# Borders between the stages of two bottleneck layers: statistics ahead and by rows, a first norm on two engines, a plain first tile, stores in parts

## The chip, the cores and the metric

The kernel runs on one core of a Trainium2 chip. Time is the device time of one execution in microseconds. The core has five engines with their own instruction streams: TensorE (PE, matmuls, with its weight loads shown as PEld), VectorE (DVE), ScalarE (ACT), GpSimd (POOL) and SyncE (SP). SP, ACT and POOL also issue DMAs. Matmuls write to eight banks of PSUM, everything else lies in SBUF or in DRAM.

## The reference

Two layers of the same form are applied to x, 64 images of 1024 channels and 14 x 14 pixels in float32. One layer is

```
out = relu(bn(conv(x,   w1, b1, 1, 0), g1, be1))    # 1x1, 1024 -> 256
out = relu(bn(conv(out, w2, b2, 1, 1), g2, be2))    # 3x3,  256 -> 256
out =      bn(conv(out, w3, b3, 1, 0), g3, be3)     # 1x1,  256 -> 1024
x   = relu(x + softplus(residual_scale)[0] * out)
```

where bn takes mean and variance over all images and pixels: gamma * (x - mean) * rsqrt(var + 1e-5) + beta. So each bn needs all of its convolution's output before its first element can be normalized.

## The kernel before

Channels lie on the 128 partitions: 1024 channels are 8 blocks (CS), 256 are 2 "slots" (MS). Pixels are cut into T = 32 tiles of two images (PX = 392 columns), and for conv2 into NG = 8 groups of eight images (1568 columns per slot). The 256 channels between the convolutions stay in SBUF for all images (`y_all`); x between the layers goes through DRAM (`mids`). A float32 matmul shows as two PE instructions in the profile.

The stages, with b the number of the layer:

1. *First stage* (b = 0): conv1, the first two tiles plainly (`plain_conv1`, L378), the others by a scheme of seven products for a 2 x 2 block multiplication (`Seven`, L170, `Conv1`, L236). `stream` (L213) orders the products p1..p7 of neighbouring tiles. DVE makes the sums t1, t2, t3 (L287 to L289) after p1 and t4 (L306) after p6; results go to `y_all` by ACT or by DVE (L279), with `bn_stats` (L282) per tile. x_0 comes in two halves.
2. *Border to conv2*: `aggregate` (L689) turns the 32 rows of statistics of each slot into mean and variance with one `bn_aggr` each, `affine` (L700 to L717) makes scale and shift: a square root on ACT, the rest small DVE operations. `norm` (L396) applies them on ACT with a relu, group by group.
3. *conv2*: in rows of images by a transform with six products (0 to 5), taken in the pairs (1,2), (3,4), (0,5) for each group. `combine` (L413 to L450) makes the inputs r of a pair and their column sums on DVE and loads transformed weights u (1280 KB) on SP's queue; `products` (L470 to L483) are the matmuls, first the one that reads `sums`; `finish` adds the results (L503, L534) and takes the `bn_stats` of the group by tiles of 392 columns when all four rows of outputs are written. `combine` of the next pair is called before `products` of this one.
4. *Border to gram*: `aggregate`, `affine`, `norm` as before; `crow`, a row of constants, is loaded by SP. For b = 0, w1 of the next layer is loaded by four issues on ACT (L109).
5. *gram* (L559): conv3's statistics are taken from Z'Z, so that conv3 need not run twice. In 49 steps of 256 columns Z is transposed on PE (L583), centred by DVE (L585), and multiplied (L571, L572). `conv3_stats` (L597) makes mean and variance of all 1024 outputs (`quad`, L632).
6. *Fused stage* (b = 0, `fused`, L649): conv3 of layer 0 by seven products (`Conv3`, L311, stream c, 28 products per tile) side by side with conv1 of layer 1 (stream a, 28 products per tile), one product of each in turn. c starts 28 + LAG = 42 products ahead. ACT copies product banks (L234), DVE adds them to x in place (L341), POOL adds others (L367), ACT applies relu and stores the tile on its own queue (L376).
7. For b = 1 conv2, gram, and then `residual` (L638) per tile: conv3 plainly, DVE (L645), ACT relu (L646), one store on POOL's queue. The first two conv3 blocks are `made` ahead of the statistics.

The order of matmuls on PE is the program's own (`keep_in_program_order`, L135). Some operations of DVE and ACT are held to it as well; the others are placed by a scheduler. Each engine works its instructions in that order; buffers come from pools, and PSUM banks carry names. In the fused stage the banks are ay (2), ap, ax for conv1 and cy (2), cp, cx for conv3. A product into a bank waits until what was in it has been read; p3 of a quad of conv3 goes into the bank cp that p5 filled, after DVE has read it (L341).

Of the kernel before, what the change touches and what calls it, by code (L numbers as in the profile page):

```python
# [21 lines left out]

# [49 lines left out]
def bottlenecks(ctx: ExitStack, tc: tile.TileContext, x, w1s, w2s, w3s, pars, out):  # L72
# [18 lines left out]
    def psum_pool(bufs=8):  # L91
        return tc.tile_pool(name="psum", bufs=bufs, space=bass.MemoryType.PSUM)
# [44 lines left out]
    def psum_tile(psum, n=PX, tag="ps", **kw):  # L137
        return psum.tile([P, 512], FP, tag=tag, name=tag, **kw)[:, :n]

# [30 lines left out]
    class Seven:  # L170
# [7 lines left out]
        def bank(self, tag, bufs=1):  # L178
            tag = self.prefix + tag
            return self.psum.tile([P, 512], FP, tag=tag, name=tag, bufs=bufs)[:, : self.n]  # L180

        def p1(self):
            self.y = self.bank("y", 2)
            yield from self.product(self.y, self.a[0][0], self.b[0][0], True)
            self.after1()
# [50 lines left out]
    class Conv1(Seven):  # L236
# [28 lines left out]
        def end(self):  # L265
            pass
# [17 lines left out]
        def after1(self):  # L284
            self.u1 = self.saved("au1")
            self.t1, self.t2, self.t3 = (self.sum(i) for i in range(1, 4))
            nc.vector.tensor_sub(self.t3, self.b[1][1], self.b[0][1])  # L287
            nc.vector.tensor_add(self.t2, self.t3, self.b[0][0])
            nc.vector.tensor_sub(self.t1, self.b[0][1], self.b[0][0])  # L289
# [88 lines left out]
    def plain_conv1(psum, t, xt, a, par, stats):  # L378

        banks = [psum_tile(psum) for o in range(MS)]  # L380
# [11 lines left out]
    def norm(g, aff):  # L392
        scale, shift = aff
        for s in range(MS):
            y = y_grp[:, s, g]
            nc.scalar.activation(y, y, AF.Relu, bias=shift[:, s : s + 1], scale=scale[:, s : s + 1])  # L396

    def conv2(psum, pool, b, par, aff, stats):
# [9 lines left out]
        def last(to, g, k, by):  # L408

            nc.scalar.activation(to[:, :, RT - 1, :], y_grp[:, :, g, 4 * (RT - 1) + k - 1, :], AF.Copy, scale=by)  # L410
# [4 lines left out]
        def combine(g, pair):  # L415

            full = RT - 1
            ra, rb = new("r"), new("r")
            if pair[0] == 1:
                t1, t2 = new("t"), new("t")  # L420
                last(t1, g, 2, -4.0)
                last(t2, g, 1, -4.0)
                for s in range(MS):
                    stt(t1[:, s, :full], rows(g, s, 2, 0, full), -4.0, rows(g, s, 4, 0, full))
                    stt(t2[:, s, :full], rows(g, s, 1, 0, full), -4.0, rows(g, s, 3, 0, full))
                nc.vector.tensor_add(ra, t1, t2)
                nc.vector.tensor_sub(rb, t1, t2)
            elif pair[0] == 3:
# [3 lines left out]
                both = slice(0, MS)  # L432
                nc.vector.tensor_sub(t3[:, :, :full], rows(g, both, 4, 0, full), rows(g, both, 2, 0, full))
                nc.vector.tensor_sub(t4[:, :, :full], rows(g, both, 3, 0, full), rows(g, both, 1, 0, full))
                stt(ra, t4, 2.0, t3)
                stt(rb, t4, -2.0, t3)
            else:
# [7 lines left out]
            made = []  # L445
            for i, r in zip(pair, (ra, rb)):
                lines = (full if i == NF - 1 else RT) * GI
                r = r.rearrange("p s r (i w) -> p s (r i) w", i=GI)[:, :, :lines]
                sums = pool.tile([P, MS, RT * GI, WH], FP, tag="sums", name="sums", bufs=BUFS["sums"])[:, :, :lines]
                nc.vector.tensor_add(sums, r[:, :, :, WH:], r[:, :, :, :WH])  # L450
                u = pool.tile([P, MS, MS, NK, P], FP, tag="u", name="u", bufs=BUFS["u"])
                nc.sync.dma_start(out=u, in_=us[b][i])
                made.append((i, lines, r, sums, u))
            return made

        def products(made):
            done = []
            for i, lines, r, sums, u in made:
# [3 lines left out]
                for o in range(MS):  # L462
                    def w(s, k):
                        return u[:, s, o, k]
# [80 lines left out]
        for k, (g, pair) in enumerate(pairs):  # L545
            if pair[0] == 1 and g + 1 < NG:
                norm(g + 1, aff)
# [318 lines left out]
```

## Time and profile before

| | us |
|---|---|
| median of 4 runs | 2213.17 (2212.88 to 2214.5) |
| the profiled execution, its time | 2214.5 |
| its span | 2212.7 |
| PE busy | 2128.6 (96%) |
| DVE busy | 1431.4 (65%) |
| ACT busy | 724.0 (33%) |
| POOL busy | 250.4 (11%) |
| mean granted TensorE clock | 0.982 |

A busy line gives an engine's time, its share of the span and its instructions. A wait line names the instruction that waited, and behind the arrow the one that released it, with total, times and longest. The chain of waits is the path of work followed back from the last instruction. A granted clock of 1.00 is full speed of TensorE. A single time such as 806.78 is counted from the start of the span.

### The profile page before, as it was taken

To read this page: it belongs to the slowest core of one execution; us is meant where nothing else is said; L and a number is where in the kernel's file an instruction comes from. 1 tells how busy PE (TensorE), PEld (TensorE's weight loads), DVE (VectorE), ACT (ScalarE), POOL (GpSimd) and SP (SyncE) were. 2 spreads that over 40 slices of the span, in tenths; PEclk is the share of its full clock that TensorE was granted. 3 is DMA by queue.
4 is the path that set the end of the run, shared out by engine and by line. 5 is a ranking of instruction groups with operands and counts; after the bars stand their busy time and mean duration, and the time that the engine had idled before them with its cause. 6 is when DMAs were issued, how large, how long until landed. Compare 5 with 4: busy or idle time off the path is not lost.

```text
span 2212.7 us, 27233 instructions
## 1 busy us (share of the span) xinstructions
PE 2128.6 (96%) x10648; PEld 1810.7 (82%) x10648; DVE 1431.4 (65%) x2591; ACT 724.0 (33%) x1391; POOL 250.4 (11%) x350
## 2 busy tenths in 40 slices
PE   8999979999998989999999999799999799999997
PEld 4555549999997879999999999699999797555554
DVE  5676557788775656676666666678878534444443
ACT  1111133111105045555555555611111221444443
POOL 0000000000001133333333333000000000000000
PEclk9999989999998989999999999899999899999999
DMA  7655425555534424444444442355555501787884
GB/s 283 251 201 202 174 96 181 187 199 184 187 137 158 153 94 170 175 175 165 165 167 175 175 175 117 148 190 191 190 187 194 195 16 55 295 292 295 306 318 185
DMA packets 44289, 409.44 MB, mean 185 GB/s; under 512 B 5504, under 2 KB 5760, under 8 KB 11392
## 3 DMA queue, kind: packets, MB, share of 16 engines
q1 hardware_dynamic: 29664, 287.06, 36.2%
q0 software_dynamic: 8448, 67.11, 7.4%
q10 hardware_dynamic: 6048, 53.52, 5.8%
q8 instruction: 84, 1.38, 0.3%
q14 instruction: 45, 0.37, 0.0%
HBM read 289.18 MB, written 118.49 MB: 184 GB/s over the span
## 4 chain that ended last, share of the span: by engine, by line
PE 73%; issue 20%; DVE 4%; DMA 2%; POOL 1%; ACT 1%; POOLq 0%; SPq 0%; ACTq 0%
PE ay L135 14%; PE cy L135 7%; PE ap L135 7%; PE ps L475 6%; PE ps L481 6%; PE ps L470 6%; PE ps L477 6%; PE ps L483 6%; PE cp L135 4%; PE ax L135 3%; PE cx L135 2%; PE bx L571 2%; PE ps L135 1%; DMA y<-in_w 1%; PE bp L572 1%
## 5 line engine op out<-in xcount | busy, mean ns | idle before, releaser
L135 PE MATMUL ps<-y,w 128*128 128x392 f32 x1024 | 339.2, 494 | 0.0
L135 PEld LDWEIGHTS ps<-y,w 128*128 128x128 f32 x1024 | 195.2, 191 | 142.8 <-issue 1.6
L645 DVE SCALAR_TENSOR_TENSOR x<-ps,scale,x 128x392 f32<-128x392 f32 x256 | 159.8, 625 | 174.2 <-PE ps L135 174.2
L234 ACT ACTIVATE cu<-cy,scale 128x196 f32<-128x196 f32 x384 | 158.4, 422 | 230.2 <-PE cy L135 227.7
L646 ACT ACTIVATE x<-x,shift 128x392 f32<-128x392 f32 x256 | 158.9, 622 | 177.5 <-DVE x L645 177.5
L135 PE MATMUL ay<-at,w1s 128*128 128x196 f32 (+1 forms) x752 | 209.7, 382 | 0.8 <-ACT au L234 0.6
L503 DVE TENSOR_TENSOR f<-ps,ms 128x448 f32<-128x448 f32 x192 | 113.3, 600 | 147.8 <-PE ps L483 80.2
L470 PE MATMUL ps<-sums,u 128*128 128x224 f32 (+1 forms) x768 | 172.1, 347 | 25.2 <-DVE sums L450 25.2
L475 PE MATMUL ps<-r,u 128*128 128x224 f32 (+1 forms) x768 | 173.6, 347 | 0.0
L481 PE MATMUL ps<-r,u 128*128 128x224 f32 (+1 forms) x768 | 172.8, 346 | 0.0
L494 ACT ACTIVATE ms<-ps 128x448 f32<-128x448 f32 (+1 forms) x80 | 41.9, 524 | 391.2 <-PE ps L470 391.2
L135 PEld LDWEIGHTS ay<-at,w1s 128*128 128x128 f32 x752 | 136.0, 190 | 36.3 <-ACT au L234 4.3
L470 PEld LDWEIGHTS ps<-sums,u 128*128 128x128 f32 x768 | 137.3, 190 | 26.2 <-ACT t L410 13.1
L234 ACT ACTIVATE x<-x,shift 128x392 f32<-128x392 f32 x256 | 145.5, 614 | 30.8 <-POOL x L367 28.9
L477 PE MATMUL ps<-r,u 128*128 128x192 f32 (+1 forms) x768 | 153.7, 321 | 0.0
L483 PE MATMUL ps<-r,u 128*128 128x192 f32 (+1 forms) x768 | 153.4, 321 | 0.0
L367 POOL TENSOR_TENSOR x<-x,cu 128x392 f32<-128x392 f32 x128 | 130.4, 1019 | 190.1 <-DVE x L341 187.8
L341 DVE SCALAR_TENSOR_TENSOR x<-cp,scale,x 128x196 f32<-128x196 f32 x256 | 106.8, 417 | 67.1 <-PE cp L135 67.1
L475 PEld LDWEIGHTS ps<-r,u 128*128 128x128 f32 x768 | 141.8, 190 | 1.3
L481 PEld LDWEIGHTS ps<-r,u 128*128 128x128 f32 x768 | 136.4, 188 | 1.4
L477 PEld LDWEIGHTS ps<-r,u 128*128 128x128 f32 x768 | 132.7, 189 | 1.2
L483 PEld LDWEIGHTS ps<-r,u 128*128 128x128 f32 x768 | 132.0, 188 | 1.1
(161 smaller groups left out, 3674.2 us busy)
## 6 DMA issues: line engine op xcount, KB each, us to landing
u<-u SPq DMA_DIRECT2D x96, 1280.0 KB, 5.5
x<-in_x SPq DMA_DIRECT2D x62, 1568.0 KB, 6.7
mid<-x ACTq DMA_DIRECT2D x32, 1568.0 KB, 5.1
x<-mid SPq DMA_DIRECT2D x32, 1568.0 KB, 8.3
out<-x POOLq DMA_DIRECT2D x32, 1568.0 KB, 8.4
u<-y POOLq DMA_DIRECT2D x24, 320.0 KB, 6.5
u<-spare POOLq DMA_DIRECT2D x24, 320.0 KB, 3.1
x<-in_x SPq DMA_DIRECT2D x4, 784.0 KB, 6.7
```

Of the source, the lines that this page charges most:

```text
L135: tc.keep_in_program_order(nc.tensor.matmul(*args, **kw))
L234: tc.keep_in_program_order(nc.scalar.activation(*args, **kw))
L341: nc.vector.scalar_tensor_tensor(v, bank, self.scale[:, o : o + 1], v, ALU.mult, ALU.add)
L367: nc.gpsimd.tensor_add(v, v, self.u12)
L470: nc.tensor.matmul(m[:, o, :n], w(s, D1D2), sums[:, s].rearrange("p l c -> p (l c)"), start=(s == 0), stop=(s == MS - 1),)
L475: nc.tensor.matmul(odd, w(s, D1), r[:, s, :, WH:], start=(s == 0), stop=False)
L477: nc.tensor.matmul(odd[:, :, : WH - 1], w(s, D3), r[:, s, :, WH + 1 :], start=False, stop=(s == MS - 1))
L481: nc.tensor.matmul(even, w(s, D2), r[:, s, :, :WH], start=(s == 0), stop=False)
L483: nc.tensor.matmul(even[:, :, 1:], w(s, D0), r[:, s, :, : WH - 1], start=False, stop=(s == MS - 1))
L503: nc.vector.tensor_tensor(f[:, o].rearrange("p r (i q c) -> p q (r i) c", i=GI, q=2)[:, :, :lines], eos[o][:, :, :n].rearrange("p q (l c) ...
L645: nc.vector.scalar_tensor_tensor(v, ps, scale[:, o : o + 1], v, ALU.mult, ALU.add)
L646: nc.scalar.activation(v, v, AF.Relu, bias=shift[:, o : o + 1])
```

## The change

It touches the places between the stages.

- PSUM banks are named and taken in a cycle (`Psum`); for b = 0 gram, the statistics and the fused stage share one set of them.
- x_0 is loaded in four parts.
- In `Conv1.after1` the subtractions t3 and t1 keep program order on DVE.
- `summarize` aggregates all but the last rows of statistics ahead of a stage's end and writes the summary in the place of one row, so that the last `bn_aggr` reads three rows (conv1 of layer 0), two (conv1 of layer 1) or five (conv2).
- `affine` has one operation fewer between square root and scale; the sign of the offset goes into the last operation but one.
- The first group's norm ahead of conv2 is one slot on ACT; of the other slot 896 elements are done on DVE and 672 on ACT. The first `combine` goes by slot, and the first item's matmuls are ordered by slot, with those that read `sums` last.
- In conv2 the `bn_stats` are taken by output row k as it is written, L503 and L534 per slot, and `combine` of (3,4) stands behind `finish` of (0,5) of the group before on DVE.
- In gram the first group's norm is cut after 256 columns.
- For b = 0 also two conv3 blocks are `made` ahead, and tile 0 of conv3 is done plainly by `residual`, its store on POOL's queue; stream c starts at tile 1, 14 products ahead.
- The last output tile is stored in four parts on SP's queue.

```diff
-    def psum_pool(bufs=8):
-        return tc.tile_pool(name="psum", bufs=bufs, space=bass.MemoryType.PSUM)
+    class Psum:
+        def __init__(self, scope, cycle, **bufs):
+            self.pool = scope.enter_context(tc.tile_pool(name="psum", bufs=1, space=bass.MemoryType.PSUM))
+            self.cycle, self.bufs = itertools.cycle(cycle), bufs
+        def tile(self, n=PX, tag=None):
+            tag = tag or next(self.cycle)
+            return self.pool.tile([P, 512], FP, tag=tag, name=tag, bufs=self.bufs.get(tag, 1))[:, :n]
...
         def end(self):
-            pass
+            if self.ts[-1] == T - 1 - len(self.ts):
+                summarize(self.stats, T // 2 - 1, T - len(self.ts), PX)
...
         def after1(self):
             self.u1 = self.saved("au1")
             self.t1, self.t2, self.t3 = (self.sum(i) for i in range(1, 4))
-            nc.vector.tensor_sub(self.t3, self.b[1][1], self.b[0][1])
+            tc.keep_in_program_order(nc.vector.tensor_sub(self.t3, self.b[1][1], self.b[0][1]))
             nc.vector.tensor_add(self.t2, self.t3, self.b[0][0])
-            nc.vector.tensor_sub(self.t1, self.b[0][1], self.b[0][0])
+            tc.keep_in_program_order(nc.vector.tensor_sub(self.t1, self.b[0][1], self.b[0][0]))
...
-    def norm(g, aff):
+    def norm(s, y, aff):
         scale, shift = aff
-        for s in range(MS):
-            y = y_grp[:, s, g]
-            nc.scalar.activation(y, y, AF.Relu, bias=shift[:, s : s + 1], scale=scale[:, s : s + 1])
+        nc.scalar.activation(y, y, AF.Relu, bias=shift[:, s : s + 1], scale=scale[:, s : s + 1])
+    def norm_vector(s, y, aff):
+        scale, shift = aff
+        nc.vector.tensor_scalar(y, y, scale[:, s : s + 1], shift[:, s : s + 1], ALU.mult, ALU.add)
+        nc.vector.tensor_scalar(y, y, 0.0, None, ALU.max)
...
+        def combine(g, pair, between=None):
             full = RT - 1
             ra, rb = new("r"), new("r")
+            made = []
+            def ready(r):
+                i = pair[len(made)]
+                lines = (full if i == NF - 1 else RT) * GI
+                r = r.rearrange("p s r (i w) -> p s (r i) w", i=GI)[:, :, :lines]
+                sums = pool.tile([P, MS, RT * GI, WH], FP, tag="sums", name="sums", bufs=BUFS["sums"])[:, :, :lines]
+                nc.vector.tensor_add(sums, r[:, :, :, WH:], r[:, :, :, :WH])
+                u = pool.tile([P, MS, MS, NK, P], FP, tag="u", name="u", bufs=BUFS["u"])
+                nc.sync.dma_start(out=u, in_=us[b][i])
+                made.append((i, lines, r, sums, u))
...
+            both = slice(0, MS)
             if pair[0] == 1:
                 t1, t2 = new("t"), new("t")
-                last(t1, g, 2, -4.0)
-                last(t2, g, 1, -4.0)
-                for s in range(MS):
-                    stt(t1[:, s, :full], rows(g, s, 2, 0, full), -4.0, rows(g, s, 4, 0, full))
-                    stt(t2[:, s, :full], rows(g, s, 1, 0, full), -4.0, rows(g, s, 3, 0, full))
-                nc.vector.tensor_add(ra, t1, t2)
+                slots = [both] if between is None else [slice(s, s + 1) for s in range(MS)]
+                for part in slots:
+                    if part.start:
+                        between()
+                    last(t1, g, 2, -4.0, part)
+                    last(t2, g, 1, -4.0, part)
+                    for s in range(part.start, part.stop):
+                        stt(t1[:, s, :full], rows(g, s, 2, 0, full), -4.0, rows(g, s, 4, 0, full))
+                        stt(t2[:, s, :full], rows(g, s, 1, 0, full), -4.0, rows(g, s, 3, 0, full))
+                    nc.vector.tensor_add(ra[:, part], t1[:, part], t2[:, part])
+                ready(ra)
                 nc.vector.tensor_sub(rb, t1, t2)
+                ready(rb)
             elif pair[0] == 3:
...
+                for t, k in ((t3, 4), (t4, 3)):
+                    ins = nc.vector.tensor_sub(
+                        t[:, :, :full], rows(g, both, k, 0, full), rows(g, both, k - 2, 0, full)
+                    )
+                    if g == 0:
+                        tc.keep_in_program_order(ins)
...
+                by_slot = first and not done
+                if by_slot:
+                    order = [(s, o, part) for s in range(MS) for o in range(MS) for part in range(4)]
+                    order += [(s, o, None) for o in range(MS) for s in range(MS)]
+                else:
+                    order = [
+                        (s, o, part) for o in range(MS) for part in (None, 0, 1, 2, 3) for s in range(MS)
+                    ]
+                for s, o, part in order:
+                    if part is None:
+                        shared(o, s)
+                    else:
+                        columns(o, s, part)
...
+            def stat(o, k):
+                nc.vector.bn_stats(stats[:, o, 4 * g + k, :], out_rows[k][:, o])
...
+                for item, f, more, k in zip(done, (fa, fb), acc, (0, 3)):
+                    n = RT if k == 0 else full
+                    for o in range(MS):
+                        column(item, f, o)
+                        nc.vector.tensor_add(out_rows[k][:, o], more[:, o, :n], f[:, o, :n])
+                        stat(o, k)
+                if g == NG - 2:
+                    summarize(stats, 4 * (NG // 2), 4 * (NG - 1), GPX // 4)
...
+        half = 8
+        norm(0, y_grp[:, 0, 0], aff)
+        norm_vector(1, y_grp[:, 1, 0, :half], aff)
+        ahead = combine(*pairs[0], lambda: norm(1, y_grp[:, 1, 0, half:], aff))
+        acc = None
         for k, (g, pair) in enumerate(pairs):
             if pair[0] == 1 and g + 1 < NG:
-                norm(g + 1, aff)
+                for s in range(MS):
+                    norm(s, y_grp[:, s, g + 1], aff)
...
+                px = [normed * GPX, (normed + 1) * GPX]
+                if normed == 0:
+                    px.insert(1, CH * P)
+                for a, b in zip(px, px[1:]):
+                    for s in range(MS):
+                        norm(s, y_all[:, s, a:b], aff)
...
-    def residual(psum, pool, b, t, w3, aff, made):
+    def residual(psum, pool, b, t, w3, aff, made=()):
         scale, shift = aff
         xt = load_x(pool, b, t)
+        to = mids[t] if b == 0 else out[t]
+        step = 2 if b == 1 and t == T - 1 else CS
         for o in range(CS):
             ps = made[o] if o < len(made) else conv3(psum, t, o, w3)
             v = xt[:, o, :]
             nc.vector.scalar_tensor_tensor(v, ps, scale[:, o : o + 1], v, ALU.mult, ALU.add)
             nc.scalar.activation(v, v, AF.Relu, bias=shift[:, o : o + 1])
-        nc.gpsimd.dma_start(out=out[t], in_=xt.rearrange("p s f -> p (s f)"))
...
-    def fused(psum, pool, xpool, w1, w3, aff, par, stats):
-        xs = [load_x(xpool, 0, 0)]
+            if (o + 1) % step == 0:
+                queue = nc.gpsimd if step == CS else nc.sync
+                queue.dma_start(
+                    out=to[:, (o + 1 - step) * PX : (o + 1) * PX],
+                    in_=xt[:, o + 1 - step : o + 1, :].rearrange("p s f -> p (s f)"),
+                )
+        return xt
+    def fused(psum, pool, xpool, first, w1, w3, aff, par, stats):
+        xs = [first, load_x(xpool, 0, 1)]
         def last_convs():
-            for t in range(T):
+            for t in range(1, T):
...
-        for i in range(step + LAG):
+        for i in range(LAG):
             next(c)
...
-    def aggregate(stats, n):
+    def summarize(stats, half, end, count):
+        n = stats.shape[1]
+        mv = small.tile([P, n, 2, nc.vector.BN_AGGR_DIM], FP, tag=f"part{n}", name="part")
+        bounds = 0, half, end
+        for o in range(n):
+            for h in range(2):
+                nc.vector.bn_aggr(
+                    mv[:, o, h, :], stats[:, o, bounds[h] : bounds[h + 1], :].rearrange("p t f -> p (t f)")
+                )
+        for h in range(2):
+            to, c = stats[:, :, end - 1, 3 * h : 3 * h + 3], float(count * (bounds[h + 1] - bounds[h]))
+            nc.vector.memset(to[:, :, 0:1], c)
+            nc.vector.tensor_copy(to[:, :, 1:2], mv[:, :, h, 0:1])
+            nc.vector.tensor_scalar(to[:, :, 2:3], mv[:, :, h, 1:2], c, None, ALU.mult)
+    def aggregate(stats, first):
+        n = stats.shape[1]
         mv = small.tile([P, n, nc.vector.BN_AGGR_DIM], FP, tag=f"mv{n}", name="mv")
         for o in range(n):
-            nc.vector.bn_aggr(mv[:, o, :], stats[:, o, :, :].rearrange("p t f -> p (t f)"))
+            nc.vector.bn_aggr(mv[:, o, :], stats[:, o, first:, :].rearrange("p t f -> p (t f)"))
...
+        nc.scalar.activation(sd, mv[:, :, 1], AF.Sqrt, bias=eps)
         nc.vector.tensor_scalar(v, mv[:, :, 1], EPS, None, ALU.add)
-        nc.scalar.activation(sd, v, AF.Sqrt)
         nc.vector.reciprocal(r, sd)
-        nc.vector.tensor_mul(q, r, r)
-        nc.vector.tensor_mul(q, q, v)
-        nc.vector.tensor_scalar(q, q, -0.5, 1.5, ALU.mult, ALU.add)
-        nc.vector.tensor_mul(r, r, q)
-        scale, shift, off = tl("scale"), tl("shift"), tl("off")
+        nc.vector.tensor_mul(q, r, v)
+        nc.vector.scalar_tensor_tensor(q, q, -0.5, r, ALU.mult, ALU.mult)
+        nc.vector.scalar_tensor_tensor(r, q, 1.5, r, ALU.add, ALU.mult)
+        scale, shift = tl("scale"), tl("shift")
         nc.vector.tensor_mul(scale, r, par[:, g : g + n])
         if conv_bias is None:
-            nc.vector.tensor_scalar(off, mv[:, :, 0], -1.0, None, ALU.mult)
+            off = mv[:, :, 0]
         else:
+            off = tl("off")
             bias = par[:, conv_bias : conv_bias + n]
             nc.vector.tensor_add(off, mv[:, :, 0], bias)
-            nc.vector.tensor_sub(off, bias, off)
-        nc.vector.tensor_mul(shift, off, scale)
+            nc.vector.tensor_sub(off, off, bias)
+        nc.vector.scalar_tensor_tensor(shift, off, -1.0, scale, ALU.mult, ALU.mult)
         nc.vector.tensor_add(shift, shift, par[:, be : be + n])
...
-        pair = [load_x(xpool, 0, t, 2) for t in range(2)]
+        pair = [load_x(xpool, 0, t, 4 if t == 0 else 2) for t in range(2)]
...
-        aff = affine(aggregate(stats1, MS), MS, pb, G1, BE1)
+        aff = affine(aggregate(stats1, T - 3 + b), MS, pb, G1, BE1)
...
-            aff = affine(aggregate(stats2, MS), MS, pb, G2, BE2)
+            aff = affine(aggregate(stats2, 4 * (NG - 1) - 1), MS, pb, G2, BE2)
             with ExitStack() as scope:
-                psum = scope.enter_context(psum_pool(5))
+                if b == 0:
+                    psum = Psum(scope, ["cy", "ay", "cx", "cy", "ay"], cy=2, ay=2)
+                else:
+                    psum = Psum(scope, ["ps"], ps=5)
...
-                    made = [conv3(psum, 0, o, w3) for o in range(2)] if b == 1 else ()
+                    made = [conv3(psum, 0, o, w3) for o in range(2)]
...
+                first = residual(psum, xpool, b, 0, w3, aff, made)
                 if b == 1:
-                    for t in range(T):
-                        residual(psum, xpool, b, t, w3, aff, made if t == 0 else ())
+                    for t in range(1, T):
+                        residual(psum, xpool, b, t, w3, aff)
                     return
-            stats1 = stats_tile(MS, f"stats1_{b + 1}")
-            with psum_pool(1) as psum, tc.tile_pool(name=f"conv1_{b + 1}", bufs=1) as pool:
-                fused(psum, pool, xpool, *weights, aff, par[b + 1], stats1)
+                stats1 = stats_tile(MS, f"stats1_{b + 1}")
+                with tc.tile_pool(name=f"conv1_{b + 1}", bufs=1) as pool:
+                    fused(psum, pool, xpool, first, *weights, aff, par[b + 1], stats1)
```

## The prediction

> **What bounds the kernel now.** I read the page first, for the bound; then the waits of TensorE (PE), for where it stands still; then the windows around those places, for the clock it gets there; then the chain of work and the timeline at each place the change touches.
>
> The page, busy time by engine:
> ```profile
> PE 2128.6 (96%) x10648; PEld 1810.7 (82%) x10648; DVE 1431.4 (65%) x2591; ACT 724.0 (33%) x1391; POOL 250.4 (11%) x350
> ```
> PE is the bound: of 2212.7 us it is idle for only 84. TensorE waits (total, times, longest):
> ```profile
> PE ps L470 <- DVE sums L450: 25.2, 2, 12.6
> PE ps L583 <- ACT y L396: 22.4, 4, 11.0
> PE ps L135 <- DMA w<-in_w: 6.6, 1, 6.6
> PE ap L135 <- DVE y L279: 5.4, 6, 1.6
> PE bx L571 <- DVE zt L585: 4.9, 5, 1.3
> PE cy L135 <- ACT cu L234: 4.5, 3, 2.9
> PE cy L135 <- DVE x L341: 2.2, 1, 2.2
> ```
> The two longest kinds are the borders: conv1 to conv2 (L470, once per layer) and conv2 to gram (L583). Windows (PE busy, PEld, DVE, ACT, POOL, then clock, DMA share, GB/s):
> ```profile
> 325.00:331.00 6.00, 5.46 (x20) 5.18 (x21) 6.00 (x11) 6.00 (x6) 0.00 (x0) 0.65 0.00 1
> 660.00:672.00 12.00, 0.99 (x6) 0.82 (x5) 8.76 (x24) 2.83 (x3) 0.20 (x4) 0.65 0.77 272
> 780.00:807.00 27.00, 20.16 (x86) 16.82 (x87) 17.93 (x52) 12.94 (x30) 9.54 (x11) 0.81 0.31 120
> 807.00:1385.00 578.00, 577.61 (x3413) 565.30 (x3412) 395.74 (x878) 311.10 (x731) 195.36 (x245) 1.00 0.42 162
> ```
> Borders run at a clock of 0.65 to 0.81; the fused stage is full: 0.4 us of 578 is idle. So time can be won at borders and lost in the fused stage. The chain at the first border (start, us):
> ```profile
> 315.98 0.17 DVE q L704
> ...
> 317.16 0.17 DVE shift L717
> ...
> 318.95 1.69 ACT y L396
> 320.66 1.34 DVE t L413 x3
> ...
> 324.90 0.55 DVE sums L450
> ...
> 325.54 1.83 PE ps L470 x4
> ```
> All is serial: two norms of 1.69, then combine, sums, PE.
>
> **The change part by part** (minus is gain; sum against the profiled execution's own 2214.5, whose span is 2212.7; the median of the runs shown, 2213.17, is 1.3 lower).
>
> 1. *Head.* PE starts at 6.62, after about 1.07 MB of weights and half of x_0. Quarters let it start after 0.66 MB; at the 325 GB/s of those slices 0.41 MB is 1.26 us. −1.2 (0 to −1.5, zero if the weights are what lands last).
>
> 2. *First stage, DVE order.* Before, sums t1, t3, t2 (0.97 each) stand ahead of the L279 that frees bank ap; after, L279 is ahead of them. Of the six L279 waits, three lie in this stage, 2.5 in all with 1.31 the longest; the last (307.49) has no tile after it and may stay in part. −1.5 (−0.5 to −2.5).
>
> 3. *Statistics and affine, layer 0.* The last matmul ends at 313.03 and shift at 317.33. One bn_aggr over 32 rows is 1.03 (L689), over 3 rows about 0.2 to 0.3 like the small ops; one step of the q chain goes (0.20 pitch). But the square root's table load on ACT ends at 314.94 (1.28 us), so sqrt gains only from 315.54. Shift at 316.55: −0.8 (−0.5 to −1.0).
>
> 4. *First norm and combine, layer 0.* From shift to PE is 8.2 us now. After: norm s=0 on ACT 1.69 (beside it DVE normalizes half of s=1: 896 elements twice, between 0.64 by the 0.286 for 256 and 0.216 for 128 elements, and the 1.08 of a two-input 896), last rows 0.4, then t1, t2, and the add for one slot, each half the size (0.6 each, partly during norm); the r products of s=0 go first. That is 3.65 us. −4.55 (−3.5 to −5). Behind it, s=1 needs 672 elements on ACT and 2 us of DVE; the 8 products of s=0 (16 instructions, at the half pitch after this restart some 0.35 each, 5.6 us) cover that. The sums products come last, so L450 leaves the path.
>
> 5. *Conv2 to gram, layer 0.* Now: last matmul 660.2, f (L503), eight bn_stats 3.84, two aggregates 1.89, affine, norm; gram's transposes at 671.21 and its first products at 674.48. After, bn_stats go by row, so all but the last rows' 2 × 0.55 are done, aggregates are 0.3, norm is of 256 columns, not 1568. DVE would be ready by about 664.5, but on ACT four w1 issues (2.06 us) stand ahead of sqrt, and crow, issued at 662.15, takes 6.5 to land (668.65). The products start near 669.5, with 7 more transposes to do (1.5 us). −3.5 (−2.5 to −4.5).
>
> 6. *Gram to fused, layer 0.* Now the first conv1 matmul is at 806.78 (gram ends 766.95; c runs 42 yields alone, first waiting 2.93 for its scale, at half clock). After: two convs "made" before the statistics, 2.63 (layer 1's own row, 1852.08 to 1854.71); statistics 10.43 (same source); so quad ends at 780.1, and scale is ready 3.1 later. Six plain convs at 1.31, +1.6 of cold pitch: 789.6. Then 14 yields and the wait for ACT's relus (1.3): 6.5 to 8. First conv1 matmul near 797.7. −9 (−6 to −11). Plain tile 0 is 10.5 of PE against 28 yields × 0.331 = 9.3; that is inside.
>
> 7. *Fused stage, the loss.* DVE's and PE's timeline of one tile:
> ```profile
> 1105.61 0.97 DVE L287 TENSOR_TENSOR at<-x 128x784 f32<-128x784 f32 x1
> 1106.62 0.97 DVE L288 TENSOR_TENSOR at<-at,x 128x784 f32<-128x784 f32 x1
> 1108.51 0.42 DVE L341 SCALAR_TENSOR_TENSOR x<-cx,scale,x 128x196 f32<-128x196 f32 x1
> 1109.35 0.42 DVE L341 SCALAR_TENSOR_TENSOR x<-cp,scale,x 128x196 f32<-128x196 f32 x1 [0.42 <-PE cp L135]
> 1110.80 0.49 PE L135 MATMUL cp<-y,w3s 128*128 128x196 f32 x2
> ```
> DVE has t1 behind it early (1104.19) and t3, t2 (L287, L288) in a slack place; it then waits for PE at cp. The program order after is: L279, cy, t3, cx, t2, t1, cp. On PE's times: cy's read at 1107.2, t3 from 1107.53 (pitch 0.90 here), cx at 1108.5, t2 1108.85, t1 1109.75, cp 1110.65, done 1111.06, seen on PE some 0.1 later. The p3 product into the same bank would be at 1110.69 without stalls. So PE stalls 0.46, and two stalls of now (0.18 together: ap at 1108.41, cp at 1115.49) go partly. Net 0.4 × 30 tiles = +12 (−3, all covered and the old stalls gone, to +20, if the three sums run at 1.0 pitch and L279 waits for ACT). Queued behind cp on DVE: L279, the second bn_stats, next cp; PE waits for those only 3 us later.
>
> 8. *End of the fused stage.* 1.61 of waiting at 1390.65 for L279 goes, as in step 2; the 1.03 at 1399.88 is the last tile's and I leave it: −1.6 (0 to −2.6).
>
> 9. *Statistics and affine, layer 1.* Shift 1407.06 is late by an aggregate that DVE does between the bn_stats (1402.54 to 1403.48), which goes, too: to 1405.72. −1.35 (−0.8 to −1.8).
>
> 10. *First norm, layer 1.* As step 4 (the wait is 12.65 against 12.52): −4.55 (−3.5 to −5).
>
> 11. *Conv2 to gram, layer 1.* As step 5, without issues on ACT: transposes at 1762.15 now, products at 1765.52. crow is issued at 1753.19 and lands 4.8 later, near 1758. Products near 1759, less 1.5 of transposes yet to do. −5.1 (−3 to −6.5).
>
> 12. *Tail.* Last relu ends 2202.83, POOL issues by 2203.65, 1568 KB land in 5.4 (DMA active 2204.2 to 2208.0 at 401 GB/s), span ends 2212.7. Only the last 392 KB remain: 0.98 of transfer instead of 3.9. −3 (−2 to −3.5).
>
> *At nothing*: conv2's inner order. DVE finishes pair (0,5), now with bn_stats in it and with 4 more instructions, before it combines (3,4). That combine is ready about 417.1 in the group around 425.0, where PE needs it: cover 7.9 us; without it the excess would be paid 14 times. Splitting L534 and L503 adds some 2 us of DVE per group, in that cover. Plain tile 0's store moves to POOL's queue once; bank names only take the place of pools.
>
> *Clock.* 806.8 to 810.4 ran at half pitch after a wait of just 2.16. [...]
>
> By the trace a cold restart is 6 us at 0.65, 2.1; my sum keeps every one, and no step gains by clock.
>
> **Sum.** Gains 1.2+1.5+0.8+4.55+3.5+9+1.6+1.35+4.55+5.1+3 = 36.15; loss 12; net −24. 2214.5 − 24 = 2190.4.
>
> **The rivals.**
> A. *No stall in the fused stage*: t2 or t1 runs early enough, in the DVE idle of 1.24 before L279. For: DVE is busy 396 of 578 there. Against: DVE obeys its written order, and cp stands behind three 0.97 sums. −36: 2178.
> B. *Borders give half*: crow, w1 issues, the u weights (1280 KB, median 7.0; issued 313.11, first landing near 318.3) or the cold clock end last. For: DMA is 0.77 busy at 660 to 672. Against: u lands before step 4's restart at 320.2. Gains 22, loss 12: 2204.
> C. *Slower*: the stall is repeated. If a p3 delay makes L279, t4 (L306) or another read late as well, each tile pays more; the place is the same queue, and it decides from 36/30 = 1.2 us net per tile. At 1.5 per tile: +45 − 36 = +9, 2223. For: POOL, ACT and DVE are all linked by single buffers. Against: after the stall DVE idles over 1 us per tile.
> D. *A cover fails in conv2*: combine (3,4) over 7.9 us late; at 10 us, 14 × 2 = +28, 2218. Against: DVE is at 65%.
>
> **How the numbers follow.** My forecast 0.48, A 0.22, B 0.18, C 0.06, D 0.02, "doesn't do what it says" (aggregates or sums unchanged in effect, near 2213) 0.04. The range that leaves out C, D, half of that and the edges is 2174 to 2206; the forecast's own, by its bounds, 2183 to 2197. A measurement of this kernel tells no more than 0.2% (4.4 us) from no change: faster is below 2208.7, that is forecast, A, and B nearly whole: 0.88; same 0.05; slower 0.07.
>
> **What would show it.** Right: in the fused stage a repeated TensorE wait of 0.4 to 0.5 on bank cp behind DVE's read, 30 times; the conv2 waits near 7 each, now for r and not sums; the gram waits at 4 to 7; some 7 us from the last relu to the end, not the 9.9 of now; first conv1 matmul some 9 us earlier relative to gram's end. Wrong: 578 us of fused stage unchanged (A); waits of conv2 over 10 or new waits on DMA (B); fused stage above 610 (C); a new L470 wait in each group (D).

## The result and the profile after

The changed kernel takes 2219.98 us (median of 34 runs, 2211.84 to 2221.24) against 2213.22 (55 runs, 2210.95 to 2215.55). The ratio, which is that of the means, is 1.002, 95% interval 1.0015 to 1.0025. It is slower by 0.2%, or 0.3% by the medians, where 2190 was forecast and 2174 to 2206 given as the range. The changed kernel's runs lie in groups: six near 2212, six near 2215, two near 2218 and twenty near 2220.5. The profiled execution is of the second group, 2215.1 with a span of 2213.3, so the table below explains a run 4.9 below the median.

TensorE's waits in the changed kernel (total, times, longest):
```profile
PE cp L144 <- DVE x L347: 20.8, 30, 0.7
PE ay L144 <- DVE at L294: 15.1, 6, 2.7
PE ps L513 <- DVE r L454: 14.1, 2, 7.3
PE cp L622 <- DVE zt L642: 6.7, 5, 2.0
PE cy L640 <- ACT y L401: 6.0, 1, 6.0
PE ps L144 <- DMA w<-in_w: 5.7, 1, 5.7
PE ps L640 <- ACT y L401: 5.3, 3, 4.6
PE ap L144 <- DVE y L285: 2.3, 2, 1.3
```
The two conv2 waits fell from 12.5 to about 7 each, and those ahead of gram from 11 to 6.0 and 4.6. In their place stand two new rows: 30 waits for DVE's read of cp (L347), which the prediction has, and six for the sum t2 (L294), which it has not.

Cut at TensorE's own marks, the two spans compare so ("predicted" adds up the prediction's steps for the stretch):

| stretch | before | after | difference | predicted |
|---|---|---|---|---|
| to the first matmul | 6.62 | 5.71 | −0.9 | −1.2 |
| first stage, to its last matmul | 306.4 | 318.4 | +12.0 | −1.5 |
| wait for conv2, layer 0 | 12.52 | 7.30 | −5.2 | −5.35 |
| conv2 to gram's first product | 348.9 | 345.7 | −3.3 | −3.5 |
| to the first conv1 matmul of the fused stage | 132.3 | 124.9 | −7.4 | −9 |
| from there to the last matmul of the fused stage | 596.0 | 619.8 | +23.8 | +10.4 |
| wait for conv2, layer 1 | 12.65 | 6.81 | −5.8 | −5.9 |
| conv2 to gram's first product | 350.1 | 343.4 | −6.7 | −5.1 |
| to the last relu's end | 437.3 | 437.7 | +0.4 | 0 |
| last relu to the end | 9.9 | 3.7 | −6.2 | −3 |
| span | 2212.7 | 2213.3 | +0.6 | −24 |

The borders gave 35.1, two more than predicted. The first stage and the fused stage lost 35.8.

**The first stage.** TensorE's timeline of the changed kernel (start, duration, and in brackets the wait and what ended it):
```profile
33.47 2.87 PE L144 MATMUL ay<-at,w1s 128*128 128x392 f32 x8 [2.26 <-DVE at L294]
54.81 2.87 PE L144 MATMUL ay<-at,w1s 128*128 128x392 f32 x8 [2.67 <-DVE at L294]
94.64 4.33 PE L144 MATMUL ay<-at,w1s 128*128 128x392 f32 x8 [2.73 <-DVE at L294]
135.93 2.87 PE L144 MATMUL ay<-at,w1s 128*128 128x392 f32 x8 [2.73 <-DVE at L294]
175.76 4.57 PE L144 MATMUL ay<-at,w1s 128*128 128x392 f32 x8 [2.73 <-DVE at L294]
318.57 2.90 PE L144 MATMUL ap<-x,w1s 128*128 128x392 f32 x8 [1.31 <-DVE y L285]
```
DVE's timeline at the third of them:
```profile
88.53 1.02 DVE L170 SCALAR_TENSOR_TENSOR y<-y 128x384 f32<-128x384 f32 x2
89.47 1.09 DVE L171 TENSOR_TENSOR y<-y 128x256 f32<-128x256 f32 x3
90.47 1.78 DVE L293 TENSOR_TENSOR at<-x 128x1568 f32<-128x1568 f32 x1
92.18 0.62 DVE L285 SCALAR_TENSOR_TENSOR y<-ap,par,au 128x392 f32<-128x392 f32 x1
92.71 1.78 DVE L294 TENSOR_TENSOR at<-at,x 128x1568 f32<-128x1568 f32 x1
```
In TensorE's timeline the last line, a wait for bank ap, was there before, too; the five waits above it are new. Beside four of the tile pairs the kernel transforms conv2's filters (L154 to L171). Now 4.7 us of that work on DVE stands ahead of t3 (L293); t2 (L294) needs t3, and product p6 needs t2. Before, t3 and t2 (L287, L288) were done first and the filters (from L148 on) after:
```profile
82.76 1.79 DVE L287 TENSOR_TENSOR at<-x 128x1568 f32<-128x1568 f32 x1 [0.84 <-PE ay L135]
85.01 1.78 DVE L288 TENSOR_TENSOR at<-at,x 128x1568 f32<-128x1568 f32 x1
87.18 0.54 DVE L148 TENSOR_TENSOR y<-y 128x384 f32<-128x384 f32 x1
```
The other wait, at 33.47, is the first seven-product pair: t3 started at 21.91 before, and starts at 29.72 now, behind the statistics of the plain tiles.

**The fused stage.** DVE's timeline of one tile:
```profile
1115.73 0.42 DVE L347 SCALAR_TENSOR_TENSOR x<-cp,scale,x 128x196 f32<-128x196 f32 x1 [1.57 <-PE cp L144]
1116.73 1.40 DVE L293 TENSOR_TENSOR at<-x 128x784 f32<-128x784 f32 x1
1118.05 0.41 DVE L347 SCALAR_TENSOR_TENSOR x<-cx,scale,x 128x196 f32<-128x196 f32 x1
1118.38 1.04 DVE L294 TENSOR_TENSOR at<-at,x 128x784 f32<-128x784 f32 x1
1119.35 0.96 DVE L295 TENSOR_TENSOR at<-x 128x784 f32<-128x784 f32 x1
1120.23 0.41 DVE L347 SCALAR_TENSOR_TENSOR x<-cp,scale,x 128x196 f32<-128x196 f32 x1
```
and POOL's in the same time:
```profile
1116.29 1.01 POOL L373 TENSOR_TENSOR x<-x,cu 128x392 f32<-128x392 f32 x1 [3.68 <-DVE x L347]
1117.26 1.34 POOL L368 TENSOR_TENSOR x<-x,cu 128x196 f32<-128x196 f32 x1
```
This is the order t3, cx, t2, t1, cp of step 7. But t3 (L293) takes 1.40, not 0.97, and POOL's L368 takes 1.34, not the 0.60 of its other instances: the two lie on each other. In the kernel before, t3 and t2 were done by 1107.6, and POOL was idle until 1108.07:
```profile
1108.07 1.01 POOL L367 TENSOR_TENSOR x<-x,cu 128x392 f32<-128x392 f32 x1 [4.68 <-DVE x L341]
```
TensorE's p3 product now waits for DVE's read of cp:
```profile
1120.70 0.60 PE L144 MATMUL cp<-y,w3s 128*128 128x196 f32 x2 [0.69 <-DVE x L347]
```
It comes 1.19 after the matmul in front of it instead of 0.33, and a tile lasts 19.68 us instead of 18.91.

### The profile page after: what moved, and what is told of

Its sections match the earlier page's. It is cut to its first block, busy times and chain, and to the rows that moved or that the text cites. A ratio compares the mean times of both kernels' runs of the same rounds, so it can differ in the third digit from the quotient of the medians.

```text
span 2213.3 us, 27276 instructions
## 1 busy us (share of the span) xinstructions
PE 2129.8 (96%) x10624; PEld 1806.9 (82%) x10624; DVE 1446.7 (65%) x2648; ACT 721.3 (33%) x1387; POOL 264.8 (12%) x342
## 4 chain that ended last, share of the span: by engine, by line
PE 86%; DVE 11%; issue 1%; ACT 1%; DMA 1%; SPq 0%; DVEq 0%; ACTq 0%
PE ps L513 23%; PE ps L144 17%; PE ay L144 13%; PE ps L494 6%; PE cy L144 6%; PE ap L144 5%; PE ax L144 4%; PE cp L144 4%; PE cp L622 4%; DVE at L293 2%; PE ap L623 2%; DVE at L294 2%; PE cx L144 2%; DVE x L347 2%; DVE at L295 1%
## 5 line engine op out<-in xcount | busy, mean ns | idle before, releaser
L513 PE MATMUL ps<-r,u 128*128 128x224 f32 (+3 forms) x3072 | 561.4, 334 | 14.1 <-DVE r L454 14.1
L513 PEld LDWEIGHTS ps<-r,u 128*128 128x128 f32 x3072 | 535.1, 189 | 19.8 <-DVE r L454 7.9
L347 DVE SCALAR_TENSOR_TENSOR x<-cp,scale,x 128x196 f32<-128x196 f32 x248 | 103.2, 416 | 105.9 <-PE cp L144 105.9
L239 ACT ACTIVATE x<-x,shift 128x392 f32<-128x392 f32 x248 | 142.9, 613 | 21.2 <-POOL x L368 19.1
L373 POOL TENSOR_TENSOR x<-x,cu 128x392 f32<-128x392 f32 x124 | 125.8, 1015 | 167.1 <-DVE x L347 165.4
L622 PE MATMUL cp<-zt 128*128 128x257 f32 x392 | 119.6, 387 | 6.9 <-DVE zt L642 6.7
L144 PE MATMUL cy<-ct,w3s 128*128 128x196 f32 x496 | 123.4, 330 | 1.4 <-ACT cu L239 1.4
L368 POOL TENSOR_TENSOR x<-x,cu 128x196 f32<-128x196 f32 x124 | 96.4, 777 | 221.5 <-DVE x L347 143.4
L239 ACT ACTIVATE au<-ay 128x196 f32<-128x196 f32 (+1 forms) x141 | 53.7, 381 | 204.2 <-PE ay L144 203.8
L144 PE MATMUL ap<-x,w1s 128*128 128x196 f32 (+1 forms) x376 | 104.6, 382 | 2.4 <-DVE y L285 2.3
L401 ACT ACTIVATE y<-y,shift,scale 128x1568 f32<-128x1568 f32 (+2 forms) x68 | 103.1, 1584 | 5.6 <-DVE shift L801 5.6
```

The costliest lines, as they stand in the source:

```text
L144: tc.keep_in_program_order(nc.tensor.matmul(*args, **kw))
L239: tc.keep_in_program_order(nc.scalar.activation(*args, **kw))
L347: nc.vector.scalar_tensor_tensor(v, bank, self.scale[:, o : o + 1], v, ALU.mult, ALU.add)
L368: nc.gpsimd.tensor_add(self.part(1, 1), self.part(1, 1), u3)
L373: nc.gpsimd.tensor_add(v, v, self.u12)
L513: nc.tensor.matmul(to, u[:, s, o, k], v, start=start, stop=stop, skip_group_check=by_slot)
```

## The experiments

**The kept order of t3 and t1, undone and done alone.** Theory: the two `keep_in_program_order` calls in `Conv1.after1` make both losses. Rival: the fused loss is from the new phase of stream c (plain tile 0, shorter lead, shared banks).

```diff
-            tc.keep_in_program_order(nc.vector.tensor_sub(self.t3, self.b[1][1], self.b[0][1]))
+            nc.vector.tensor_sub(self.t3, self.b[1][1], self.b[0][1])
             nc.vector.tensor_add(self.t2, self.t3, self.b[0][0])
-            tc.keep_in_program_order(nc.vector.tensor_sub(self.t1, self.b[0][1], self.b[0][0]))
+            nc.vector.tensor_sub(self.t1, self.b[0][1], self.b[0][0])
```

> The changed kernel with t3 and t1 of Conv1 placed by the scheduler again. Order theory (the kept DVE order costs 11.9 us net in the first stage, where t2 stands behind the filter work four times, and 23.8 in the fused stage, where DVE's read of cp stands behind three sums): 2215.1 - 35.7, about 2179 to 2181, no wait of PE for L294, waits on cp under 0.1 each. Phase rival (the fused loss comes from the plain first tile, the shorter lead of stream c or the shared banks): about 2203, the 30 waits on cp stay.

Measured: 2178.47 (2177.47 to 2178.78), ratio to before 0.9839 (0.9825 to 0.9854). TensorE's waits:
```profile
PE ps L513 <- DVE r L454: 14.1, 2, 7.3
PE ap L144 <- DVE y L285: 5.3, 5, 1.6
PE cp L144 <- DVE x L347: 0.3, 1, 0.3
```
Both new rows are gone, the borders' gains stay, and a tile of the fused stage lasts 18.90 again. The theory holds; the rival falls.

Next, kept in one stage alone; `len(self.ts)` is 2 in the first stage and 1 in the fused stage:
```diff
+            hold = tc.keep_in_program_order if len(self.ts) == 2 else (lambda ins: ins)
-            tc.keep_in_program_order(nc.vector.tensor_sub(self.t3, self.b[1][1], self.b[0][1]))
+            hold(nc.vector.tensor_sub(self.t3, self.b[1][1], self.b[0][1]))
```
(t1 likewise; the other kernel has `== 1`.)

> The changed kernel with t3 and t1 kept in program order in the first stage alone. Order theory: first stage as in the changed kernel, four waits of 2.7 and one of 2.3 for t2, fused stage free of the 30 waits: 2215.1 - 23.8 = 2191. Phase rival: 2215 to 2220 as the changed kernel.

> The changed kernel with t3 and t1 kept in program order in the fused stage alone. Order theory: the 13.1 us of waits for t2 in the first stage go, the 30 waits on cp stay: 2215.1 - 11.9 = 2203, up to 2208 if the spread between runs of the changed kernel (2212 to 2221) lies in the fused stage. Phase rival: the same 2203 to 2208. If the spread lies in the first stage, runs fall together within 2 us here and spread in the run with the order kept in the first stage alone.

Kept in the first stage alone: 2196.09 (2190.85 to 2196.89); five waits for t2:
```profile
PE ay L144 <- DVE at L295: 13.1, 5, 2.7
PE cp L144 <- DVE x L348: 0.3, 1, 0.3
```
Kept in the fused stage alone: 2199.67 (2198.50 to 2201.13):
```profile
PE cp L144 <- DVE x L348: 20.8, 30, 0.7
PE ay L144 <- DVE at L295: 2.0, 1, 2.0
```
Over the 2178.5 without either, the first stage costs 17.6, more than the 11.9 expected, and the fused stage 21.2. The two make 38.8, and 2217 with both, between the changed kernel's low and high runs. The first of the two kernels spreads over 6.0 us, the second over 2.6.

The same calls added to the kernel before, nothing else changed:

> The kernel before with t3 and t1 of Conv1 kept in program order and nothing else changed. Order theory: the first stage gains about 12 us of waits for t2 and the fused stage some 24 for cp: 2213.2 + 36 = 2249, with 30 waits of 0.5 to 0.7 on cp. Phase rival: 2213.2 + 12 = 2225, no waits on cp.

Measured: 2251.29 (2250.08 to 2252.38), ratio 1.0169 (1.0154 to 1.0184); TensorE's waits:
```profile
PE cp L135 <- DVE x L341: 21.3, 31, 1.0
PE ay L135 <- DVE at L288: 15.4, 6, 2.7
```
It is 38 us slower than without the calls. The loss needs nothing of the rest of the change.

**Which of the two calls.** Each run undoes one of the two lines of the first diff.

> The changed kernel with t3 alone kept in program order, t1 free. Theory of the sum of three (DVE's read of cp is late because t3, t2 and t1 all stand ahead of it): t1 moves ahead of them, the read ends 0.88 earlier, more than the 0.69 of the stall, so no wait on cp above 0.1; the four waits for t2 of 2.7 in the first stage stay: 2191 to 2197, as with the order kept in the first stage alone (2196). Rival (t3 alone, standing after L285, makes the fused loss): the 30 waits stay, 2212 to 2220.

> The changed kernel with t1 alone kept, t3 free; in the fused stage DVE's order is then t3, t2, cp, t1, L285, cy, cx, cp. Theory of the sum of three: the first stage has no wait for t2; in the fused stage the read of cp is in time but L285, which PE's bank ap needs and which stands 0.15 from its limit now, comes 0.9 later: some 30 waits on ap of 0.8 to 1.0 instead of those on cp, 2178.5 + 25 = 2203. Rival (only t3's place costs): no waits of either kind, 2178.

t3 alone kept: 2190.68 (four runs: 2185.2 and 2185.5, 2195.9 and 2196.0). The t2 waits are there (15.2 in six), no wait on cp. t3 still takes 1.40 here, so its slowness alone makes no stall. t1 alone kept: 2209.69 (2207.71 to 2210.83):
```profile
PE ap L144 <- DVE y L285: 29.3, 33, 2.2
PE ay L144 <- ACT au L239: 5.8, 6, 1.2
```
No wait for t2 and none on cp worth naming, but 33 on ap: L285 now stands behind three sums. So it needs three sums in line in the fused stage; the read that stands behind the third pays, cp or ap. The mechanism is the expected one, the cost nearly 7 us above it. In the first stage t3's place is enough.

From the first conv1 matmul of the fused stage to conv2, t3 alone kept took 598.3, neither kept 601.7.

**The size of the stall.** Theory: t3 is slow because POOL works at the same time. This kernel leaves out POOL's two additions, and with them a part of conv3's products:
```diff
-            nc.gpsimd.tensor_add(self.part(1, 1), self.part(1, 1), u3)
+            pass
...
-            nc.gpsimd.tensor_add(v, v, self.u12)
+            pass
```

> The changed kernel without GpSimd's two additions per quad in the fused stage (u3 and u12 are not added to x, so part of conv3's products of layer 0 is left out). If t3 takes 1.40 us and not 0.97 because GpSimd reads and writes SBUF at the same time, t3 falls to 0.97 here and the stall on cp from 0.69 to 0.26, about the stall that the order alone makes: 30 x 0.43 = 13 less than the changed kernel, 2199 to 2208. If the 1.40 has another cause, t3 and the 30 waits stay as they are and the time is 2212 to 2221. If GpSimd's work is the whole cause of the stall, no wait is left and the time is near 2197.

Measured: 2206.94 (2202.41 to 2210.08). TensorE's wait on cp:
```profile
PE cp L144 <- DVE x L347: 8.8, 30, 0.3
```
t3's group in the fused stage (count, busy, mean ns), first in the changed kernel:
```profile
L293 DVE TENSOR_TENSOR at<-x 128x784 f32<-128x784 f32 x28 | 39.2, 1399 | 0.0
```
then without POOL's additions:
```profile
L293 DVE TENSOR_TENSOR at<-x 128x784 f32<-128x784 f32 x28 | 27.0, 965 | 0.0
```
A tile lasts 19.28, 0.37 more than before; the changed kernel's 0.77 is that and 0.40 from the overlap. t3, with two inputs from SBUF, goes from 965 to 1399 ns under POOL's additions, while L347, with one input from PSUM, takes 0.41 beside L368 in the timeline above and 0.41 to 0.42 away from POOL's additions. Where such a sum and an addition of POOL overlap here, the one that starts later is slowed. Above, L373 starts 0.44 ahead of t3 and keeps its 1.01, and L368 starts 0.53 behind t3 and takes 1.34. With t1 alone kept, t1 starts 0.22 ahead of L373; there t1 keeps its 0.96, and L373 takes 1.62.

**The spread of the runs.** A wait is called cold here if half clock follows it, a granted clock of 0.50 (in the profile above from 94.17 to 97.58, for one). In the first timeline above the eight matmuls behind a wait of 2.7 take 2.87 or 4.33 to 4.57. Windows behind the second, third and fourth wait of the changed kernel (the clock is the third number from the end):
```profile
54.80:60.20 5.40, 5.39 (x17) 3.17 (x18) 4.53 (x5) 1.02 (x2) 0.54 (x1) 1.00 0.99 398
94.60:100.00 5.40, 5.36 (x12) 3.13 (x13) 4.57 (x5) 0.80 (x2) 0.53 (x1) 0.72 0.98 382
135.90:141.30 5.40, 5.37 (x17) 3.17 (x18) 4.22 (x4) 0.50 (x1) 0.00 (x0) 1.00 0.79 311
```
The same wait is followed by full clock or not. A second profile of the same kernel:

> The changed kernel, a second profile. Clock theory of the spread of its runs (2211.8 to 2221.2): the five waits of 2.3 to 2.7 for t2 in the first stage sometimes end in 3.4 us at half clock and sometimes not, each costing 1.7 to 2.1. The first profile has 2 of 5 and 2215.1. So this one has n of 5 and 2211 + 2.1 n, within 1. Rival: the spread lies elsewhere, and n does not go with the time.

Measured 2218.08; TensorE's timeline:
```profile
35.00 4.57 PE L144 MATMUL ay<-at,w1s 128*128 128x392 f32 x8 [2.26 <-DVE at L294]
58.03 2.87 PE L144 MATMUL ay<-at,w1s 128*128 128x392 f32 x8 [2.67 <-DVE at L294]
97.86 2.87 PE L144 MATMUL ay<-at,w1s 128*128 128x392 f32 x8 [2.72 <-DVE at L294]
137.69 4.56 PE L144 MATMUL ay<-at,w1s 128*128 128x392 f32 x8 [2.73 <-DVE at L294]
179.21 4.47 PE L144 MATMUL ay<-at,w1s 128*128 128x392 f32 x8 [2.73 <-DVE at L294]
```
Three of five are cold, and the time is 2218.1, where 2217.3 within 1 was expected. From the first of these waits to conv2's start it is 297.9 with two cold ones, 299.8 with three, 301.3 with four (order kept in the first stage alone) and 303.0 with five (the kernel without POOL's additions, whose first stage is the same): 1.7 each, not 2.1. So of the 3.0 between the two profiles 1.8 lies there. Another 1.4 lies ahead of the first wait: the half clock at the program's start lasts until 8.84 in one and 11.78 in the other (in the first profile a matmul takes 0.90 on average between 6.6 and 8.4 and 0.49 from 9.4 on). Five waits cost 13.1 by themselves and up to 8.5 more by the clock. That can make most of the changed kernel's spread of 9.4, but only two of its runs were profiled. In these profiles the half clock behind such a wait lasts 3.41 each time, and its starts lie whole multiples of that apart (94.17 and 176.09, 24 times 3.413). What decides between the two outcomes was not shown; the length of the wait alone does not, as the second profile has half clock behind 2.26 at 35.00 and the first has none behind 2.73 at 135.93. Left open: the 10.8 between the runs with t3 alone kept. Its profile, a low run, has two cold waits already, so three more explain 5.1, and the wait of 2.04 in the fused stage, not cold there, 1.7.

**The tail.** One store instead of four, or four on POOL's queue, both with t3 and t1 free:
```diff
-        step = 2 if b == 1 and t == T - 1 else CS
+        step = CS
...
-                queue = nc.gpsimd if step == CS else nc.sync
+                queue = nc.sync if b == 1 and t == T - 1 else nc.gpsimd
```
```diff
-                queue = nc.gpsimd if step == CS else nc.sync
+                queue = nc.gpsimd
```

> The changed kernel with t3 and t1 free, and the last tile stored by one DMA of 1568 KB on SP's queue. From the last relu to the end it was 9.9 before (one DMA on POOL's queue) and 3.7 after (four on SP's). Theory of bytes alone (step 12): 2.9 of that comes back, and the rest too, 2178.5 + 6 = 2184.5. Theory that bytes give 2.9 and the queue 3.3: 2181.4.

> The changed kernel with t3 and t1 free, and the last tile stored in four parts on POOL's queue. Theory of bytes alone: no change, 2178.5. Theory that bytes give 2.9 and the queue 3.3: 2181.8, with some 7 us from the last relu to the end, as step 12 had it.

Measured: 2180.38 and 2182.10, against 2178.47. From the last relu's end to the end of the span:

| | SP's queue | POOL's queue |
|---|---|---|
| four parts | 3.7 | 8.5 |
| one part | 6.9 | 9.9 (kernel before) |

Smaller last parts save 3.1 on SP's queue and 1.4 on POOL's; the queue saves 3.0 with one part and 4.8 with four. The two do not add up as the expectation had it, but about half of the tail's gain of 6.2, or more, is the queue. The medians moved by less than the tails, by 1.9 and 3.6. Landing from the issue is 5.1 on SP's queue against 5.4 on POOL's for one part. From the landing to the end of the span it is 1.7 against 4.2, and 1.1 against 5.6 with four parts. So most of the queue's difference lies after the data landed; what is done there was not measured.

**Step 5's limit, and a version that beats both.** crow loaded at the start of each layer, w1 of layer 1 issued by SP (`small` has one buffer instead of two, for room), t3 and t1 free:
```diff
-                    crow = pool.tile([P, M], FP, tag="crow", name="crow")
-                    nc.sync.dma_start(out=crow, in_=pars[b][:, NPAR:])
...
+        crow = keep.tile([P, M], FP, tag="crow", name="crow")
+        nc.sync.dma_start(out=crow, in_=pars[b][:, NPAR:])
...
-                nc.scalar.dma_start(out=w[:, o, h], in_=w1s[b][:, o, h])
+                (nc.scalar if b == 0 else nc.sync).dma_start(out=w[:, o, h], in_=w1s[b][:, o, h])
```

> The changed kernel with t3 and t1 free, and crow loaded at the start of each layer rather than at the border, and the next layer's w1 issued by SP rather than by ACT. Step 5's reading (at layer 0's border the square root stands behind ACT's four issues and the first product behind crow): sqrt 1.3 us earlier, wait for zt gone (1.8), products 2 to 3 us earlier, some 1 us of it given back in transposes not yet done: 2178.5 - 2 = 2176.5. Rival (cold clock and norm set the start anyway): 2178 to 2179.

Measured: 2175.77 (2174.06 to 2176.18), 2.7 less. TensorE's wait for the first norm is 4.68 instead of 6.03, and gram's first product follows the first transposes by 2.2, not 4.0. Step 5 named the right limits; the two edits were made together, so what each is worth alone rests on these two waits.

Then t3 kept in the fused stage alone, t1 free:
```diff
-            nc.vector.tensor_sub(self.t3, self.b[1][1], self.b[0][1])
+            t3 = nc.vector.tensor_sub(self.t3, self.b[1][1], self.b[0][1])
+            if len(self.ts) == 1:
+                tc.keep_in_program_order(t3)
...
```

> The version with crow early and w1 issued by SP, with t3 alone kept in program order in the fused stage (t1 free there, both free in the first stage). With t3 alone kept the fused stage took 598.3 from its first conv1 matmul to conv2, with none kept 601.7, as five waits for L285 became two and the small stalls of each tile went. So 2175.8 - 3.4 = 2172.4. If that 3.4 was a matter of the run and not of the order: 2175.8.

Measured: 2169.95 (2168.94 to 2171.36), ratio to before 0.9807 (0.9792 to 0.9822). The page's first lines:
```profile
span 2167.1 us, 27220 instructions
...
PE 2119.5 (98%) x10624; PEld 1802.1 (83%) x10624; DVE 1444.7 (67%) x2648; ACT 722.4 (33%) x1389; POOL 265.0 (12%) x342
```
The fused stage took 598.35 to conv2's start against 601.63, so the 3.3 of t3's place is repeated. Another 1.5 of the 5.8 lies between conv2's start and gram's first product of layer 1 (341.1 against 342.6); what makes it was not tried.

## Why the prediction was wrong

The failed steps are 2 and 7.

*Step 2* costed the new DVE order at −1.5 by looking at who had waited, L279, and not at who was moved back. t3 and t2 were put behind whatever DVE holds at that place; beside four pairs that is the filter work. It is +12.0 in the profile and 17.6 by the run with the first stage alone kept. I named no cover for the sums I moved there, though the trace of before had the filter work in view. The step also priced each sum at 0.97, which is the fused stage's form; in the first stage one takes 1.78.

*Step 7* had the place, the bank, the count of 30 and the sign. Its net 0.4 per tile is near what the run without POOL's additions shows (0.37), partly by luck, as the wait itself is 0.29 there and not 0.46. The term that was mis-sized is t3's 0.97: it was taken where POOL was idle, and the new place is under POOL's two additions, 1.40. The net is 0.77 per tile, 23 us, just over the range's +20 and below rival C's 1.2.

*Rival A*, 2178, is what the kernel takes without the two calls: 2178.5. But A expected no stall with the calls in place, and that failed. It also counted the 3.1 of steps 2 and 8, and with the calls undone the waits of L285 are back (5.3 in five). So the sum of the borders was nearly right, partly by cancelling, and the agreement with 2178 is luck in part: the tail gave 6.2 instead of 3 (step 12 did not count the queue), the fused stage's start 7.4 instead of 9 (step 6). The 1.5 of transposes given back, which step 5 put at its own border, may be part of the latter; that was not tested.

*Steps 1, 3 with 4, 5, 9 with 10, and 11* came out within 1.7. *Step 8* can't be seen by itself: the 1.61 is gone, but the stage has a new wait of 2.04 for t2 at 807.29, with half clock behind it (0.50 for 3.41 us from 807.56). *At nothing*: conv2's inner order cost nothing that the table shows; rival D did not occur. *Rival B*: u and crow did not take the gains, though crow and the issues held back 2.7 of layer 0's border. *Rival C*: its sign, a fused stage above 610, was met (619.8), and its 2223 lies near the measured 2220. Its mechanism was not met: the stall did not spread within the tile, and no other read made a repeated wait. The rest of the loss is step 2's.

*Clock*: I kept each cold restart at the borders and gave new waits none; the waits of step 2 brought two and three more in the changed kernel's two profiles.

## What to carry to other kernels

An instruction moved in one engine's order should be costed at every place where that order occurs, with what stands in front of it there: the two calls made no wait beside the ordinary tile pairs of the first stage and one of 2.7 us beside each of four. A duration holds for its neighbours: here a VectorE sum of two SBUF tensors slowed from 0.97 to 1.40 us under GpSimd's additions. When a change of many parts comes out near zero, undoing the one part that works in the steady state tells more than the borders do: here 35 us of gain hid 36 us of loss.

## What the runs showed of the hardware

- Of TensorE's five waits of 2.3 to 2.7 us for t2 in the first stage, two have half clock behind them in the changed kernel's first profile (0.50 granted, for 3.41 us) and three in its second; the wait of 2.0 us in the fused stage has it in the first profile, too. Such a cold wait cost up to 1.7 us: the eight matmuls behind the one at 175.76 took 4.57 instead of 2.87. None of the twelve waits of 1.0 to 1.6 us in the profile of the kernel before and the first of the changed kernel has half clock behind it.
- A VectorE add of two SBUF tensors and a GpSimd add slowed each other where they overlapped in these traces, and the one that started later paid: 0.97 to 1.40 us for VectorE's, 0.60 to 1.34 or 1.01 to 1.62 for GpSimd's.
- A last store of 1568 KB on SP's queue ended the program 3.0 us sooner than one on POOL's (6.9 against 9.9 from the last relu's end), though they landed 5.1 and 5.4 us after their issues; in four parts SP's queue was 4.8 ahead (3.7 against 8.5).
